# A two-layer graph network on one core: x reaches its feature-major form through VectorE, the leftover table through SyncE, both cosine tables through one pass

## The chip, the core and the metric

The kernel runs on one core of a Trainium2 chip. The metric is device time in microseconds (us), from start to end of one execution. Six queues matter here: TensorE multiplies matrices (PE in the profile; PEld is its weight load), VectorE (DVE) and ScalarE (ACT) do elementwise work and empty PSUM, GpSimd (POOL) does small elementwise work, SyncE (SP) issues most of the transfers, and 16 DMA engines carry them out. Each engine takes its instructions in a fixed order, and waits where the next one's inputs are not ready.

## The reference

128 graphs of 128 nodes with 256 features pass two layers. Only the first layer and the convolution of the second touch the change.

```python
# layer 0, x: (128 graphs, 128 nodes, 256 features), adj: (128, 128, 128)
norm  = (sum(adj, -1) + 1e-6) ** -0.5
f_hom = adj @ ((x @ theta) * norm) * norm
f_het = x @ W_h
gate  = sigmoid(x @ W_t + b_t)
x1    = layernorm(x + elu(gate * f_hom + (1 - gate) * f_het))
# layer 1
h      = relu(bn1(conv1(x1)))            # 1 tap
h      = bn2(conv2(h))                   # 17 taps along the nodes, padded by 8
x_conv = relu(h + x1)
...                                      # messages, GRU
out    = layernorm(x1 + gru(x_conv, x_nmp, x1))
```

All values are float32.

## The kernel before

The program has three stages. Stage A (lines 512 to 606) computes layer 0, conv1 and the analysis half of conv2, for 64 pairs of graphs (J = 2 graphs each). Stage B (line 702 on) multiplies by the transformed conv2 weights, stage C (line 1012 on) does the rest of layer 1. The change lies in stage A and in what is set up ahead of it.

Conv2 is done by a cosine and sine transform of length L = 136. `table` (L182) fills one table of 128x136 values per call with some twenty VectorE instructions: table A over the nodes, which the analysis (`l1_analyse`, L404) multiplies by, and table T over the taps, which turns the conv2 weights in `w_unit` (L420). The weights go through in 32 w_units of 8 features, each from four loads of 17 partitions (`w_load`, L124). The last 8 table columns ("leftovers") go another way: `way_back` (L234) copies them into tile TL in 14 small transfers, and 19 v_units (`v_unit`, L453) multiply by TL.

The stage is a software pipeline. One pass of the loop at L512, called a step here, does for pair t: `l0_project` (three products of x), the gate and elu of pair t-1, the layer norm of pair t-1 (`l0_norm`), the transposition, conv1 and analysis of the normalised x1 of pairs t-2 and t-3, and at its end `l0_turn(t+1)`, which prepares the next pair. Two units of the weights (w or v) fit into most steps; some steps have none: of the 61 steps from pair 3 on about 31 have a w_unit, 18 a v_unit, 12 neither.

A product over the features needs x with the features on the partitions. `load` (L114) brings x with the nodes on the partitions, 128 partitions of two rows of 1 KB. `l0_turn` (L293) calls `transposed` (L281): TensorE multiplies four 128x128 blocks of x by the identity into a PSUM bank, and VectorE copies the bank (128x512) to xT. After that come two transposes of the adjacency (L299), their row sum on VectorE (L301), and the power -1/2 on GpSimd (L160, L161). xT has one buffer: it is written for pair t+1 when the products of pair t have been read. The same node-major x is read again by `l0_elu` (L368) as the residual.

The order within an engine is that of the program text for TensorE always, and from step 3 on for SyncE, VectorE and ScalarE as well (`manual_schedule`, L513); for steps before that, a scheduler chooses theirs at build time, and GpSimd's always. `norm_stats` (L258) ends in two small GpSimd instructions (`inv_sqrt`) that ScalarE's normalisation (L273) needs.

```python
def transposed(src, dst, name):
    t = bank(f"{name}_ps")
    for c in range(NC):
        for j in range(J):
            nc.tensor.transpose(t[:, ...], src[:, j, c * P : (c + 1) * P], ident)
    nc.vector.tensor_copy(dst.rearrange("p c n -> p (c n)"), t)
```

Of the kernel before, what the change touches and what calls it, by code (L numbers as in the profile page):

```python
# [34 lines left out]
def gnn_layers_kernel(ctx: ExitStack, tc: tile.TileContext, a: dict, out: bass.AP):  # L35
# [47 lines left out]
    taps = actx.enter_context(tc.tile_pool(name="taps", bufs=1, side="right", reuse_waits="tile"))  # L83
    acon = actx.enter_context(tc.tile_pool(name="acon", bufs=1, side="right", reuse_waits="tile"))
    w0 = acon.tile([P, NC, 3 * D], F32, tag="w0", name="w0")
    A = acon.tile([P, M], F32, tag="A", name="A")
    S = const.tile([P, P], F32, tag="S", name="S")
    SL = const.tile([P, P], F32, tag="SL", name="SL")
    T = taps.tile([P, M], F32, tag="T", name="T")
    FS = P // TAPS  # L90
    TL = taps.tile([P, P], F32, tag="TL", name="TL")
    conv1_w = acon.tile([P, NC, D + CO], F32, tag="conv1_w", name="conv1_w")
    shift1 = acon.tile([P, D], F32, tag="shift1", name="shift1")
    NW = 3
    vt = [taps.tile([P, 2, D], F32, tag=f"vt{i}", name=f"vt{i}") for i in range(2)]
    wt = [taps.tile([P, 2, D], F32, tag=f"wt{i}", name=f"wt{i}") for i in range(NW)]
# [12 lines left out]
    def bank(name):  # L109
        return ps.tile([P, 512], F32, tag="ps", name=name)  # L110
# [2 lines left out]

    def load(p):  # L114
        s = st[p] = {}
        s["x"] = io.tile([P, J, D], F32, tag="x", name=f"x_{p}")
        nc.sync.dma_start(s["x"], x[p * J : (p + 1) * J].rearrange("b n d -> n b d"))
        s["adjT"] = io.tile([P, J, P], F32, tag="adjT", name=f"adjT_{p}")
        nc.sync.dma_start(s["adjT"], adjT[:, p * J : (p + 1) * J, :])

    QF = D // 4
    NU = QF // 2
# [9 lines left out]

    load(0)
    for j, name in enumerate(("L0_gnn_theta", "L0_gnn_W_h", "L0_gnn_W_t")):
        (nc.sync if j == 2 else nc.scalar).dma_start(
            w0[:, :, j * D : (j + 1) * D], a[name].rearrange("(c p) e -> p c e", p=P)
        )
    def rows(name, lo, hi, pool=acon):

        t = pool.tile([P, hi - lo], F32, tag=f"{name}{lo}", name=f"{name}{lo}_b")  # L140
# [38 lines left out]
    lag = as_float("lag", 1, quarters, [[0, 1]], -PAD, 1)  # L179
    step = 2.0 * math.pi / L  # L180

    def table(dst, at, name):  # L182


        def tmp(q, dt=F32):
            return setup.tile([P, M], dt, tag=f"{name}_{q}", name=f"{name}_{q}")

        v = nc.vector
        arg, r, u, w, acc = (tmp(q) for q in ("arg", "r", "u", "w", "acc"))
        turns = tmp("turns", I32)  # L190
        v.scalar_tensor_tensor(arg, freq, at, quad, ALU.mult, ALU.subtract)
        v.tensor_scalar(turns, arg, 1.0 / L, None, ALU.mult)
        v.tensor_copy(u, turns)
        v.scalar_tensor_tensor(r, u, float(-L), arg, ALU.mult, ALU.add)
        v.scalar_tensor_tensor(u, r, -1.0, r, ALU.mult, ALU.max)
        v.tensor_scalar(r, u, -1.0, float(L), ALU.mult, ALU.add)
        v.tensor_tensor(u, u, r, ALU.min)

        v.tensor_scalar(r, u, float(L // 4), -step, ALU.subtract, ALU.mult)
        v.tensor_mul(w, r, r)  # L200
        co = [(-1.0) ** i / math.factorial(2 * i + 1) for i in range(9)]
        v.tensor_scalar(acc, w, co[8], None, ALU.mult)
        for i in range(7, 0, -1):
            v.scalar_tensor_tensor(acc, acc, co[i], w, ALU.add, ALU.mult)
        v.scalar_tensor_tensor(dst, acc, 1.0, r, ALU.add, ALU.mult)


    scale = const.tile([P, 2 * NC], F32, tag="scale", name="scale")
# [25 lines left out]
    def way_back():  # L234

        AL = setup.tile([P, P // ML, ML], F32, tag="AL", name="AL")
        nc.vector.tensor_copy(AL, A[:, P:M].unsqueeze(1).to_broadcast([P, P // ML, ML]))
        nc.vector.memset(TL, 0.0)

        for t in vt:  # L240
            nc.vector.memset(t[96:], 0.0)
        back = setup.tile([P, 1], F32, tag="back", name="back")
        nc.vector.memset(back, 2.0 / L)
        nc.vector.memset(back[0:2], 1.0 / L)

        cols = TL[:, 0 : ML * FS].rearrange("p (r i k) -> p r i k", r=2, i=FS)
        for i in range(FS):
            for r in range(2):
                nc.gpsimd.dma_start(
                    cols[i * TAPS : (i + 1) * TAPS, r, i, :], T[0:TAPS, P + r : M : 2]  # L250
                )
        tS = bank("S_ps")
        nc.tensor.transpose(tS[:, 0:P], A[:, 0:P], ident)
        nc.tensor.transpose(tS[:, P : 2 * P], AL.rearrange("p a b -> p (a b)"), ident)
        nc.vector.tensor_scalar(S, tS[:, 0:P], back, None, ALU.mult)
        nc.vector.tensor_scalar(SL, tS[:, P : 2 * P], 2.0 / L, None, ALU.mult)

    def norm_stats(src, n, name):  # L258

# [26 lines left out]
                nc.tensor.transpose(  # L286
                    t[:, (c * J + j) * P : (c * J + j + 1) * P],
                    src[:, j, c * P : (c + 1) * P], ident,
                )
        nc.vector.tensor_copy(dst.rearrange("p c n -> p (c n)"), t)  # L290


    def l0_turn(p):  # L293
        s = st[p]
        s["xT"] = wf.tile([P, NC, J * P], F32, tag="xT", name=f"xT_{p}")
        transposed(s["x"], s["xT"], f"xT_{p}")
        adj = bank(f"adj_ps_{p}")
        for j in range(J):
            nc.tensor.transpose(adj[:, nodes(j)], s["adjT"][:, j, :], ident)  # L299
# [176 lines left out]
    m_in = []  # L476

    def m_load(i):
        t = io.tile([P, J, D], F32, tag="x", name=f"mx1T_{i}").rearrange("p j d -> p (j d)")
# [23 lines left out]
        return add, send  # L503


    units = {2 + u * (NP - 3) // (NU - 1): u for u in range(NU)}
    rest = [t for t in range(4, NP - 1) if t not in units]
    units_v = {rest[v * (len(rest) - 1) // (NV - 1)]: v for v in range(NV)}
# [3 lines left out]
    for t in range(-1, NP):  # L512
        with tc.manual_schedule(engines={E.PE, E.SP, E.DVE, E.Activation} if t > 2 else {E.PE}):  # L513

            def on(q, work):
                if 0 <= q < NP:
                    work(q)

            def between():
                on(t - 1, l0_gate)  # L520
                on(t - 3, l1_analyse)

            def beside():
                on(t - 1, l0_elu)

            on(t - 2, l1_turn)
            l0_project(t, between, beside) if t >= 0 else between()
            on(t - 1, l0_norm)
            if t == 0:
                norms = batch_norms()  # L530
                next(norms)
                table(A, node, "A")
                table(T, lag, "T")

                cos, sin = T[:, 2:M:2], T[:, 3:M:2]
                both = setup.tile([P, M // 2 - 1], F32, tag="both", name="both")
                nc.vector.tensor_sub(both, sin, cos)
                nc.vector.scalar_tensor_tensor(sin, sin, -1.0, cos, ALU.mult, ALU.subtract)
                nc.vector.tensor_copy(cos, both)
            on(t - 2, l1_front)  # L540
            on(t - 2, l1_store)
            if t + 2 < NP:
                if 2 <= t + 2:
                    load(t + 2)
                if 0 <= t < 2:
                    w_load(t)
                if 2 <= t < 4:
                    v_load(t - 2)
            else:
                m_load(t + 2 - NP)  # L550
            if t - 1 in units:
                w_store(units[t - 1])
            if t - 1 in units_v:
                v_store(units_v[t - 1])
            on(t + 1, l0_turn)
            if t == 3:
                nc.scalar.dma_start(w_msg, a["w_msgT"].rearrange("(c p) e -> p c e", p=P))
                nc.scalar.dma_start(b_msg, a["L1_gnn_b_msg"].partition_broadcast(P))
            if t == 1:
                next(norms, None)  # L560
                way_back()
                sctx.close()
                hpool = hstack.enter_context(tc.tile_pool(name="hpool", bufs=1))
                H = hpool.tile([P, NC, M, NB], F32, tag="H", name="H")
            on(t, l0_mix)
            if t in units_v:
                v_unit(units_v[t])
                if units_v[t] + 2 < NV:
                    v_load(units_v[t] + 2)
            if t in units:  # L570
                if units[t] + 2 < NU:
                    w_load(units[t] + 2)
                if t + 1 < NP:
                    w_unit(units[t])
# [511 lines left out]
```

## Time and profile before

| | |
|---|---|
| time, median of 3 runs (lowest to highest) | 2027.63 us (2027.56 to 2027.9) |
| the profiled execution: its own time, its span | 2027.4 us, 2025.6 us |
| stage A, by the last conv1 and analysis before the first product of stage B | 0 to about 715 us |
| TensorE, VectorE, ScalarE, GpSimd busy, share of the span | 98%, 72%, 37%, 32% |
| DMA packets, bytes | 198043, 243.02 MB |
| idle time of TensorE with a named cause, the two longest | 11.1 us, 4.4 us |

The span is what the profiler saw between the first and the last instruction; 1.8 us of the execution lie around it, and the profiled execution stands 0.2 us below the median. Busy time of TensorE is modelled at its end, since its instructions overlap, so that 98% says that it hardly ever waits and not that it works at its peak. In the timeline, an entry such as "x4" is four instructions in a row; its start is that of the first, and the next entry's start tells more of the pace than its own duration does.

### The profile page before, as it was taken

To read this page: it belongs to the slowest core of one execution; us is meant where nothing else is said; L and a number is where in the kernel's file an instruction comes from. 1 tells how busy PE (TensorE), PEld (TensorE's weight loads), DVE (VectorE), ACT (ScalarE), POOL (GpSimd) and SP (SyncE) were. 2 spreads that over 40 slices of the span, in tenths; PEclk is the share of its full clock that TensorE was granted. 3 is DMA by queue.
4 is the path that set the end of the run, shared out by engine and by line. 5 is a ranking of instruction groups with operands and counts; after the bars stand their busy time and mean duration, and the time that the engine had idled before them with its cause. 6 is when DMAs were issued, how large, how long until landed. Compare 5 with 4: busy or idle time off the path is not lost.

```text
span 2025.6 us, 26703 instructions
## 1 busy us (share of the span) xinstructions
PE 1993.2 (98%) x8679; PEld 1372.1 (68%) x8679; DVE 1461.8 (72%) x2884; ACT 746.2 (37%) x1488; POOL 645.5 (32%) x869
## 2 busy tenths in 40 slices
PE   6999999999999999999999999999999999999997
PEld 4676677677676788886666666666666666666664
DVE  6878878788788764456777677777767677776766
ACT  2565665656656611122223222222223222232222
POOL 4111111111111145543434243233424333343431
PEclk8999999999999999999999999999999999999999
DMA  5544444444443489983222122222221221221100
GB/s 102 178 160 155 141 162 149 153 159 148 158 153 132 152 301 351 324 292 118 68 69 80 61 66 80 63 64 64 80 69 58 80 78 49 65 79 47 42 27 21
DMA packets 198043, 243.02 MB, mean 120 GB/s; under 512 B 16768, under 2 KB 141456, under 8 KB 197904
## 3 DMA queue, kind: packets, MB, share of 16 engines
q1 hardware_dynamic: 190880, 235.47, 35.4%
q10 hardware_dynamic: 6352, 5.78, 0.9%
q0 software_dynamic: 672, 0.06, 0.5%
q8 instruction: 70, 1.15, 0.2%
q14 instruction: 69, 0.57, 0.1%
HBM read 136.33 MB, written 104.86 MB: 119 GB/s over the span
## 4 chain that ended last, share of the span: by engine, by line
PE 96%; DVE 1%; POOL 1%; DMA 0%; ACT 0%; issue 0%; SPq 0%; POOLq 0%; DVEq 0%; ACTq 0%
PE g_ps L970 42%; PE f_ps L319 11%; PE y_ps L711 6%; PE gate_ps L324 5%; PE conv_ps L389 5%; PE msg_ps L847 5%; PE coef_ps L409 3%; PE nmp_ps L903 3%; PE conv_ps L811 3%; PE z_ps L724 3%; PE mix_ps L345 3%; PE w_ps L425 2%; PE x1T_ps L286 2%; PE xT_ps L286 1%; PE conv_ps L818 1%; PE wl_ps L456 1%
## 5 line engine op out<-in xcount | busy, mean ns | idle before, releaser
L319 PE MATMUL f_ps<-w,xT 128*128 128x512 f32 x512 | 243.8, 599 | 0.4 <-DVE xT L290 0.4
L160 POOL TENSOR_SCALAR rstd_b<-mv_b 128x2 f32<-128x2 f32 (+1 forms) x65 | 12.5, 192 | 529.9 <-DVE mv_b L264 529.9
L929 ACT ACTIVATE o<-o 128x1024 f32<-128x1024 f32 (+1 forms) x65 | 67.8, 1044 | 268.5 <-DVE o L1006 261.7
L970 PE MATMUL g_ps<-t_h,sh 128*128 128x384 f32 x384 | 156.8, 490 | 0.0
L970 PE MATMUL g_ps<-t_c,sc 128*128 128x384 f32 x384 | 155.2, 486 | 0.0
L970 PE MATMUL g_ps<-t_m,sm 128*128 128x384 f32 x384 | 155.2, 486 | 0.0
L273 ACT ACTIVATE y<-y,nb_b,rstd_b 128x256 f32<-128x256 f32 x128 | 70.0, 593 | 219.0 <-DVE nb_b L271 215.1
L324 PEld LDWEIGHTS gate_ps<-w,xT 128*128 128x128 f32 x512 | 97.8, 191 | 68.6 <-issue 61.9
L160 POOL TENSOR_SCALAR rstd_a<-mv_a 128x2 f32<-128x2 f32 x64 | 12.3, 192 | 403.8 <-DVE mv_a L264 282.7
L324 PE MATMUL gate_ps<-w,xT 128*128 128x256 f32 x512 | 131.9, 380 | 0.0
L319 PEld LDWEIGHTS f_ps<-w,xT 128*128 128x128 f32 x512 | 88.8, 192 | 63.5 <-issue 62.3
L1003 POOL TENSOR_TENSOR u<-u,p 128x512 f32<-128x512 f32 x63 | 79.8, 1267 | 162.4 <-DVE p L987 162.4
L711 PE MATMUL y_ps<-wb,H 128*128 128x256 f32 x544 | 128.5, 379 | 0.8 <-issue 0.8
L328 ACT ACTIVATE hom<-f_ps,norm 128x256 f32<-128x256 f32 x128 | 60.7, 474 | 168.7 <-PE f_ps L319 166.0
L389 PE MATMUL conv_ps<-conv_w,x1T 128*128 128x259 f32 x512 | 122.5, 381 | 0.0
L719 POOL TENSOR_TENSOR ws<-wb 128x512 f32<-128x512 f32 x67 | 93.6, 1397 | 89.8 <-PE z_ps L724 51.5
L711 PEld LDWEIGHTS y_ps<-wb,H 128*128 128x128 f32 x544 | 103.2, 190 | 15.2 <-issue 1.3
L847 PE MATMUL msg_ps<-w_msg,cx1T 128*128 128x256 f32 x480 | 108.7, 379 | 0.0
L970 PEld LDWEIGHTS g_ps<-t_c,sc 128*128 128x128 f32 x384 | 73.0, 190 | 50.9
L970 PEld LDWEIGHTS g_ps<-t_m,sm 128*128 128x128 f32 x384 | 73.0, 190 | 50.9
L389 PEld LDWEIGHTS conv_ps<-conv_w,x1T 128*128 128x128 f32 x512 | 97.1, 190 | 14.7 <-ACT w_o L429 0.2
L970 PE MATMUL g_ps<-w_hhT_w,cx1T 128*128 128x384 f32 x256 | 105.1, 492 | 0.0
(229 smaller groups left out, 4515.4 us busy)
## 6 DMA issues: line engine op xcount, KB each, us to landing
wb<-w_d SPq DMA_DIRECT2D x68, 512.0 KB
w_d<-w_o SPq DMA_DIRECT2D x256, 128.0 KB
y_d<-yb SPq DMA_DIRECT2D x68, 256.0 KB
x<-in_x SPq DMA_DIRECT2D x64, 256.0 KB
cx1T<-x1T_d SPq DMA_DIRECT2D x64, 256.0 KB
yt<-y_d SPq DMA_DIRECT2D x32, 512.0 KB
cx<-x_d SPq DMA_DIRECT2D x32, 512.0 KB
x_d<-x SPq DMA_DIRECT2D x63, 256.0 KB
```

The costliest lines, as they stand in the source:

```text
L273: nc.scalar.activation(dst[:, q, :], src[:, q, :], AF.Identity, bias=nb[:, q : q + 1], scale=rstd[:, q : q + 1],)
L286: nc.tensor.transpose(t[:, (c * J + j) * P : (c * J + j + 1) * P], src[:, j, c * P : (c + 1) * P], ident,)
L319: nc.tensor.matmul(pf, lhsT=xT[:, c, nodes(j)], rhs=w0[:, c, 0 : 2 * D], start=(c == 0), stop=(c == NC - 1),)
L324: nc.tensor.matmul(pg[:, j * D : (j + 1) * D], lhsT=xT[:, c, nodes(j)], rhs=w0[:, c, 2 * D : 3 * D], start=(c == 0), stop=(c == NC - 1),)
L345: nc.tensor.matmul(pm[:, j * D : (j + 1) * D], lhsT=adjT_[:, j, :], rhs=hom[:, j, :], start=True, stop=True,)
L389: nc.tensor.matmul(ph[:, 0 : D + CO], lhsT=s["x1T"][:, c, nodes(j)], rhs=conv1_w[:, c, :], start=(c == 0), stop=(c == NC - 1),)
L711: nc.tensor.matmul(py[:, blk, :], lhsT=coefs(blk if k == 0 else 2 * k + 1 - blk, c), rhs=w[:, c, blk, :], start=(c == 0), stop=(c == NC - 1),)
L719: nc.gpsimd.tensor_tensor(ws, w[:, :, 0, :], w[:, :, 1, :], ALU.add)
L847: nc.tensor.matmul(pm[:, j * D : (j + 1) * D], lhsT=x1T[:, c, nodes(q)], rhs=w_msg[:, c, :], start=(c == 0), stop=(c == NC - 1),)
L929: nc.scalar.activation(rz, rz, AF.Tanh, scale=0.5)
L970: nc.tensor.matmul(pg[:, lo : lo + 3 * P], lhsT=s[f"f{kind}"][i][:, pr, :], rhs=factors[kind][i], start=(k == 0), stop=(k == 2), skip_grou ...
L1003: nc.gpsimd.tensor_tensor(u4, u2, p5, add)
```

## The change

x is loaded a second way. `load` now makes a tile xb: four transfers, one for each 64 features, each to 32 partitions, put on partition i of the quarter q the 64 features of every node whose number is i modulo 32 (8 pieces of 64 values, 256 bytes each, per partition). One VectorE instruction transposes the 32x32 blocks of xb into xT; TensorE's four transposes, the PSUM bank and the copy are gone from `l0_turn`. The feature that comes to lie on a partition is another than before, so the rows of w0 (theta, W_h, W_t) are placed to match, by four transfers for each weight in place of one. The node-major x, which `l0_elu` still reads, is loaded by `load_x` at step t, two steps later than before. xb and x have two buffers each in place of four of x.

A and T become two halves of one tile AT2 and are filled by one chain of VectorE instructions over 272 columns; the first instruction alone is done twice. `l0_turn(1)` moves ahead of the table in the text. The 14 transfers to TL leave `way_back` and GpSimd's queue: SyncE issues 7 in step 2 and 7 in step 3 (`leftover_table`). Seven products of a tile of ones come at the very start of TensorE's order.

```diff
-    A = acon.tile([P, M], F32, tag="A", name="A")
+    AT2 = acon.tile([P, 2, M], F32, tag="AT2", name="AT2")
+    A, T = AT2[:, 0, :], AT2[:, 1, :]
-    T = taps.tile([P, M], F32, tag="T", name="T")
+    K, Q = 32, P // 32
+    WARM = 7
...
     def load(p):
         s = st[p] = {}
-        s["x"] = io.tile([P, J, D], F32, tag="x", name=f"x_{p}")
-        nc.sync.dma_start(s["x"], x[p * J : (p + 1) * J].rearrange("b n d -> n b d"))
+        xb = s["xb"] = io.tile([P, J * Q, 2 * K], F32, tag="xb", bufs=2, name=f"xb_{p}")
+        for q in range(Q):
+            nc.sync.dma_start(
+                xb[q * K : (q + 1) * K],
+                x[p * J : (p + 1) * J, :, 2 * K * q : 2 * K * (q + 1)].rearrange(
+                    "b (r i) d -> i (b r) d", i=K
+                ),
+            )
         s["adjT"] = io.tile([P, J, P], F32, tag="adjT", name=f"adjT_{p}")
         nc.sync.dma_start(s["adjT"], adjT[:, p * J : (p + 1) * J, :])
+
+    def load_x(p):
+        s = st[p]
+        s["x"] = io.tile([P, J, D], F32, tag="x", bufs=2, name=f"x_{p}")
+        nc.sync.dma_start(s["x"], x[p * J : (p + 1) * J].rearrange("b n d -> n b d"))
...
-        (nc.sync if j == 2 else nc.scalar).dma_start(
-            w0[:, :, j * D : (j + 1) * D], a[name].rearrange("(c p) e -> p c e", p=P)
-        )
+        for q in range(Q):
+            (nc.sync if j == 2 else nc.scalar).dma_start(
+                w0[q * K : (q + 1) * K, :, j * D : (j + 1) * D],
+                a[name][2 * K * q : 2 * K * (q + 1)].rearrange("(c i) e -> i c e", i=K),
+            )
...
-        v.scalar_tensor_tensor(arg, freq, at, quad, ALU.mult, ALU.subtract)
+        for k, at in enumerate(ats):
+            v.scalar_tensor_tensor(parts[:, k, :], freq, at, quad, ALU.mult, ALU.subtract)
...
-        cols = TL[:, 0 : ML * FS].rearrange("p (r i k) -> p r i k", r=2, i=FS)
-        for i in range(FS):
-            for r in range(2):
-                nc.gpsimd.dma_start(
-                    cols[i * TAPS : (i + 1) * TAPS, r, i, :], T[0:TAPS, P + r : M : 2]
-                )
+    def leftover_table(half):
+        cols = TL[:, 0 : ML * FS].rearrange("p (r i k) -> p r i k", r=2, i=FS)
+        for i in range(FS):
+            nc.sync.dma_start(
+                cols[i * TAPS : (i + 1) * TAPS, half, i, :], T[0:TAPS, P + half : M : 2]
+            )
...
-        transposed(s["x"], s["xT"], f"xT_{p}")
+        nc.vector.transpose(
+            s["xT"].rearrange("p c (b i) -> p c b i", i=K),
+            s["xb"].rearrange("p b (c i) -> p c b i", c=NC),
+        )
...
+    warm = bank("warm_ps")
+    for _ in range(WARM):
+        nc.tensor.matmul(warm[:, 0:P], lhsT=ones, rhs=ones, start=True, stop=True)
...
-                table(A, node, "A")
-                table(T, lag, "T")
+                l0_turn(1)
+                table(AT2, (node, lag))
...
+            if t >= 0:
+                load_x(t)
             if t + 2 < NP:
...
                 if 2 <= t < 4:
+                    leftover_table(t - 2)
                     v_load(t - 2)
...
-            on(t + 1, l0_turn)
+            if t != 0:
+                on(t + 1, l0_turn)
```

More of the change, by code (lines that the diff above doesn't have):

```diff
@@ L180, in gnn_layers_kernel, with table @@
     step = 2.0 * math.pi / L
-    def table(dst, at, name):
+    def table(dst, ats):
         def tmp(q, dt=F32):
-            return setup.tile([P, M], dt, tag=f"{name}_{q}", name=f"{name}_{q}")
+            t = setup.tile([P, len(ats), M], dt, tag=f"table_{q}", name=f"table_{q}")
+            return t.rearrange("p k m -> p (k m)"), t
         v = nc.vector
-        arg, r, u, w, acc = (tmp(q) for q in ("arg", "r", "u", "w", "acc"))
-        turns = tmp("turns", I32)
-        v.scalar_tensor_tensor(arg, freq, at, quad, ALU.mult, ALU.subtract)
+        (arg, parts), (r, _), (u, _), (w, _), (acc, _) = (
+            tmp(q) for q in ("arg", "r", "u", "w", "acc")
+        )
+        turns, _ = tmp("turns", I32)
+        for k, at in enumerate(ats):
+            v.scalar_tensor_tensor(parts[:, k, :], freq, at, quad, ALU.mult, ALU.subtract)
         v.tensor_scalar(turns, arg, 1.0 / L, None, ALU.mult)
@@ L204, in table @@
             v.scalar_tensor_tensor(acc, acc, co[i], w, ALU.add, ALU.mult)
-        v.scalar_tensor_tensor(dst, acc, 1.0, r, ALU.add, ALU.mult)
+        v.scalar_tensor_tensor(
+            dst.rearrange("p k m -> p (k m)"), acc, 1.0, r, ALU.add, ALU.mult
+        )
     scale = const.tile([P, 2 * NC], F32, tag="scale", name="scale")
@@ L256, in way_back @@
         nc.vector.tensor_scalar(SL, tS[:, P : 2 * P], 2.0 / L, None, ALU.mult)
+    def leftover_table(half):
[3 more added lines that the diff above has]
+                cols[i * TAPS : (i + 1) * TAPS, half, i, :], T[0:TAPS, P + half : M : 2]
+            )
     def norm_stats(src, n, name):
@@ L295, in l0_turn @@
         s["xT"] = wf.tile([P, NC, J * P], F32, tag="xT", name=f"xT_{p}")
-        transposed(s["x"], s["xT"], f"xT_{p}")
+        nc.vector.transpose(
+            s["xT"].rearrange("p c (b i) -> p c b i", i=K),
+            s["xb"].rearrange("p b (c i) -> p c b i", c=NC),
+        )
         adj = bank(f"adj_ps_{p}")
@@ L478, in m_load @@
     def m_load(i):
-        t = io.tile([P, J, D], F32, tag="x", name=f"mx1T_{i}").rearrange("p j d -> p (j d)")
+        t = io.tile([P, J, D], F32, tag=("xb", "x")[i // 2], bufs=2, name=f"mx1T_{i}")
+        t = t.rearrange("p j d -> p (j d)")
         nc.sync.dma_start(t.rearrange("p (c n) -> p c n", c=NC), x1T_d[EP[i]])
```

## The prediction

> **What bounds the kernel now.** I read the waits of TensorE first. They name, in order, what was waited for, the total us, how often, the longest.
>
> ```profile
> PE x1T_ps L286 <- ACT x L273: 11.6, 3, 11.1
> PE xT_ps L286 <- DMA x<-in_x: 4.4, 1, 4.4
> ```
>
> TensorE waits for almost nothing but one gap of 11.1 us. Everywhere else its own instructions set the time, so an instruction taken from it is worth its pace. The timeline around the gap shows whose fault it is.
>
> ```profile
> 16.85 14.90 POOL L249 DMA_DIRECT2D TL<-T  x14
> 31.83 0.19 POOL L160 TENSOR_SCALAR rstd_a<-mv_a 128x2 f32<-128x2 f32 x1
> 32.85 0.16 DVE L271 SCALAR_TENSOR_TENSOR nb_a<-mv_a,rstd_a 128x2 f32<-128x2 f32 x1 [8.87 <-POOL rstd_a L161]
> 33.05 1.09 ACT L273 ACTIVATE x<-hom,nb_a,rstd_a 128x256 f32<-128x256 f32 x2 [10.11 <-DVE nb_a L271]
> 33.70 1.40 PE L286 MATMUL x1T_ps<-ident,x 128*128 128x128 f32 x4 [11.09 <-ACT x L273]
> 34.89 3.62 PE L319 MATMUL f_ps<-w,xT 128*128 128x512 f32 x4
> ```
>
> GpSimd issues the 14 TL transfers for 14.9 us, and the first layer norm's rstd_a stands behind them. After the gap TensorE is slow too: four f_ps products take 3.42 us start to start against 1.72 in a settled step. Third, a settled step, one without a weight unit, where x1T comes soonest:
>
> ```profile
> 109.42 0.60 PE L286 MATMUL xT_ps<-ident,x 128*128 128x128 f32 x4
> 109.62 0.42 DVE L393 TENSOR_TENSOR h<-conv_ps,shift 128x256 f32<-128x256 f32 x1 [0.38 <-PE conv_ps L389]
> 109.86 0.38 PE L299 MATMUL adj_ps<-ident,adjT 128*128 128x128 f32 x2
> 110.06 0.69 DVE L290 COPY xT<-xT_ps 128x512 f32<-128x512 f32 x1
> ...
> 111.38 1.88 PE L319 MATMUL f_ps<-w,xT 128*128 128x512 f32 x4
> ```
>
> The four transposes hold TensorE 0.44 us (109.42 to 109.86). The copy starts when VectorE has finished h, not when the transposes end, and finishes at 110.75; f_ps follows at 111.38, so 0.63 us is to spare. The stretches of three successive steps (no unit, w_unit, v_unit) give busy time by engine, granted clock and DMA share:
>
> ```profile
> 110.06:119.86 9.80, 9.80 (x48) 7.25 (x47) 8.26 (x19) 5.35 (x14) 1.77 (x4) 1.00 0.32 105
> 119.86:130.87 11.01, 11.01 (x56) 7.47 (x55) 8.41 (x18) 7.52 (x18) 1.77 (x4) 1.00 0.55 184
> 130.87:141.53 10.66, 10.66 (x50) 7.63 (x49) 8.98 (x19) 5.45 (x14) 1.77 (x4) 1.00 0.40 123
> 45.48:685.78 640.30, 640.30 (x3042) 447.93 (x3041) 513.05 (x1099) 388.73 (x903) 106.08 (x240) 1.00 0.47 154
> ```
>
> TensorE is full in each; VectorE, the third figure, is the next one.
>
> **The transposes in the settled part.** From pair 3 on, 61 steps lose four TensorE transposes at 0.109 us each: 61 x 0.436 = **26.6 us**. The mean step falls from 640.3 / 60 = 10.67 to 10.23 us (no unit 9.36, w 10.58, v 10.22).
>
> **The VectorE transpose** takes the copy's place in VectorE's order. No row shows one. From below: L361, 433 ns, a 128x512 pass from SBUF. From above: the set-up row L227 does one 128x128 shape in 0.28 to 0.87 us, a factor 3.1, which on 0.69 gives 2.15. I take **0.69**, that of the copy it replaces and of most 128x512 passes here (676 to 692). VectorE's own need per step is its busy time plus two waits that don't shrink with TensorE's work: 0.70 for the exp (L362) and up to 0.52 for rstd. That is 8.26 + 0.70 + 0.52 = 9.48 without a unit, 8.41 + 0.70 + 0.18 = 9.3 with a w, 8.98 + 0.70 + 0.33 = 10.0 with a v; over 12, 31 and 18 steps the mean is 9.54. TensorE's 10.23 stays above it. Only the steps without a unit come within 0.1 us, and their slack ahead of f_ps shrinks from 0.63 to 0.63 - 0.44 = 0.19, so nothing stalls. If the transpose takes 0.69 + d, VectorE becomes the bound at d = 0.69 (1.38 us), and every 0.1 us beyond costs 6.1 us.
>
> The page "VectorE: DVE Perf Modes" (section The three transpose paths) gives 311 ns for a 128x128 two-byte block on VectorE and recommends TensorE for such a size; no row here shows either. Four times 311 ns are an estimate of 1.24 us, by which the steps without a unit would run 0.64 us over TensorE's 9.36, some 5 us in all after their slack, and the sum would be about 2000.
>
> **The transfers of xb.** 1024 pieces of 256 bytes per step, 64 on each of 16 DMA engines. The records of the trace in stage A have 46 ns (median) for 1024 bytes, 85 for 2048, 9 for 4; later 27 for 512. A line through them gives 18 ns for 256 bytes. From above: q0, the TL queue, took 0.5% of 16 engines for 672 packets, 241 ns each.
>
> ```profile
> q1 hardware_dynamic: 190880, 235.47, 35.4%
> q0 software_dynamic: 672, 0.06, 0.5%
> ```
>
> At 18 ns it is 1.15 us per engine and step on top of 0.47 x 10.67 = 5.0, of 10.23: hidden. It would bound the step at (10.23 - 5.0) / 64 = 82 ns per piece. At 241 ns a step would be 5.0 + 15.4 = 20.4 us. I take 18, since sizes on either side of 256 lie on that line and q0 was filled by GpSimd one small transfer at a time.
>
> The page "DMA: Bandwidth & Descriptors" (Specifications) sets 512 bytes as the least size at line rate, below which a transfer reads, modifies and writes. No row shows such a doubling; an estimate of 36 ns from it leaves 7.3 us of 10.23, and the same sum.
>
> SyncE's queue issues four more DMAs per step, at 0.42 for x: 1.7 us. Past them move adjT, the w_d stores, wt and the x_d store of the next step. In a w step the stores end near 322.3 and x_d is issued at 323.53; it becomes some 0.5 us late, which nobody feels within the 10 us until x1 is overwritten. With a v_unit, SyncE is free for 1.2 us ahead of x_d. xb is issued a whole step ahead of its reader; x for the elu is now issued about 12 us ahead. With less lead than 3 us a late x would stop VectorE at L368, and behind it the layer norm. The TL transfers, 7 in each of two steps at 0.33 (the shortest SyncE issue) to 1.07 us (GpSimd's), hold SyncE 2.3 to 7.5 us, where it stands idle from 36.2 to 46.7 now.
>
> **The set-up.** On VectorE the order of the changed program is: xT(0), the table, the gate of pair 0, T's three finishing steps, diag and scale, xT(1). A table instruction over 136 columns takes 298 ns; from the 128x256 and 128x512 rows (0.42, 0.69) a column costs 1.06 ns, so 272 columns take 0.44. A and T alternated at 0.21 each, so a pair cost 0.42: the merge saves nothing. It costs, because in the old order xT(1) came out at 13.83 amid the table and now comes last. Working: xb(0) lands near 5.0 (x landed at 4.45; three more issues at 0.45 while the weights share the engines), xT(0) 5.7, two first instructions and the row sum 6.7, 18 chained ones at 0.36 to 0.44 (7.6) 14.3, gate 15.0, col, the 1.3 of GpSimd's scale and the diag rows 17.8, xT(1) 18.5. The products of pair 1 run 5.1 us to 23.7. In their shadow VectorE does hom (0.9), three gate rows (1.8), exp (0.9), elu (1.4), stats and gate of pair 1 to 26.4; rstd 1.0, nb 0.2, ScalarE's first half 0.6 with its hand-over: x1T of pair 0 at 28.4 in place of 33.70. **5.3 us** gained. Bounds: 2 us if the four-piece loads of x and w0 (six more issues ahead of ScalarE's table load, 2.7 us) are late by 3; 8 if xT(1) overlaps the table after all.
>
> The gap on TensorE shrinks from 11.1 to about 2.9 us. After the long one TensorE lost 3.0 us over x1T, f and gate (0.76 + 1.71 + 0.54); the granted clock from 20 to 40 us was 0.66. After a wait of 1.82 us near 710 the same kind of product ran at its usual pace. 2.9 lies between: half, **1.5 us**. WARM's seven products fill TensorE's first 4.45 us, in which it waits; if xb came earlier than they end, they would cost up to 3 us. No engine after 715 us sees the change.
>
> **Sum.** Against the profiled span: 2025.6 - 26.6 - 5.3 - 1.5 = 1992.2; I allow 1 us for steps without a unit in which VectorE's 0.1 us add up: 1993. What lies around the span (1.8) and the 0.2 to the median go on top: **1995 us**.
>
> **The rivals.** *VectorE fills up* (the transpose takes 1.2 to 1.5 us). For it: 80% busy now. Against: every comparable row is 0.69. At 1.24 it costs 5 us, at 1.5 some 9 us: 2000 to 2004. *The set-up gives nothing* (18 chained instructions and late loads eat the 6.8 us): 2027.6 - 26.6 + 1 = 2002. For it: xT(1) does fall 4.7 us back. Against: rstd no longer stands behind 14.9 us. *Slower, by a slow transpose*: at 2.15 us, the upper bound, VectorE needs 9.54 + 1.46 = 11.0 per step against 10.67 now, 61 x 0.33 = 20 us more, less 5 of the set-up: 2043; it decides from 1.93 us on. For it: the L227 spread, and a permuted read. Against: that spread appears only in set-up. *Slower, by the pieces*, from 82 ns on: at 100 ns a step is 11.4, 2067; least likely.
>
> **How the numbers follow.** Forecast 0.62, VectorE filling up 0.16, set-up giving nothing 0.10, slow transpose 0.08, slow pieces 0.04. The likeliest alone runs from 1991 (set-up 8, the full 3.0 of the clock) to 1999 (set-up 2, no clock). With the two middle rivals the range is 1990 to 2004. A measurement of this kernel tells 0.2% (4 us) from no change; the two slower cases hold 0.12, of which 0.02 would end within 4 us; faster 0.87.
>
> **What would show it.** Right: no xT_ps on TensorE, a step of 9.4, 10.2 and 10.6 us, a VectorE transpose near 0.69, x1T of pair 0 near 28 us, no 11 us gap. Wrong: f_ps waiting for VectorE's xT in most steps (the transpose is slow), xT waiting for a DMA (the pieces), or x1T of pair 0 after 32 us.

## The result, and the profile after

The changed kernel takes **2045.08 us** (median; 2041.69 to 2046.67, 4 runs) against 2027.6 for the kernel before on the same chip: a ratio of 1.0085, 95% interval 1.0067 to 1.0102. It is 17 us slower, where 33 us less were forecast. The profiled execution took 2044.01 us, its span is 2042.2, the mean granted clock 0.992 (before: 0.995).

The chain of work that ended last, of the kernel after (its shares by engine):

```profile
PE 85%; DMA 7%; DVE 3%; ACT 3%; SPq 1%; issue 1%; POOL 0%; ACTq 0%; POOLq 0%; DVEq 0%
```

A store now sets part of the end. The waits (us in total, times, longest) name it: the store of x1 to memory, x_d.

```profile
ACT x L298 <- DMA x_d<-x: 49.0, 24, 7.7
PE x1T_ps L311 <- ACT x L298: 36.1, 19, 9.9
PE f_ps L347 <- DVE xT L321: 3.1, 1, 3.1
```

x1 has one buffer. ScalarE's norm of a pair (L298) may write it only when the x1 of the pair before has been stored; TensorE's transposes of x1 wait for the norm. The VectorE transpose (last line) delays TensorE once, at the start. One stalled step, from the timeline of the kernel after (start us, duration us; in brackets the idle time before and what ended it):

```profile
283.24 1.67 SPq L143 DMA_DIRECT2D wt<-in_conv_wT  x4
285.02 1.02 SPq L429 DMA_DIRECT2D x_d<-x  x1
286.14 0.37 SPq L430 DMA_DIRECT2D x1T_d<-x1T  x1
...
288.38 0.16 DVE L296 SCALAR_TENSOR_TENSOR nb_a<-mv_a,rstd_a 128x2 f32<-128x2 f32 x1 [0.18 <-POOL rstd_a L179]
289.60 0.70 DVE L321 STREAM_TRANSPOSE xT<-xb 128x512 f32<-128x512 f32 x1
292.47 1.09 ACT L298 ACTIVATE x<-hom,nb_a,rstd_a 128x256 f32<-128x256 f32 x2 [3.61 <-DMA x_d<-x]
293.12 0.33 PE L311 MATMUL x1T_ps<-ident,x 128*128 128x128 f32 x1 [2.82 <-ACT x L298]
```

The previous norm ended at 280.78. Its store was issued 4.2 us later, at 285.02, behind the four loads of convolution weights (wt), and the next norm, whose inputs were there at 288.54, got x1 at 292.4. The chain of waits in this stretch has the store itself:

```profile
285.02 7.37 DMA x_d<-x
```

Why does a store of 256 KB take 7.37 us? The records of the DMA packets, counted by size for each microsecond of the kernel after, tell. wt moves in 136 packets of 1 KB, x_d and x1T_d in 128 packets of 2 KB each.

```
from us        283  284  285  286  287  288  289  290  291  292
1024 bytes      54    8   17   23   23  252   29   21    5   33
2048 bytes       0    0    0   79  161    0    0    0   10    6
```

At 286 and 287 the 1 KB packets come at 23 per us, one every 43 ns, and such a packet takes 46 ns: **one DMA engine** carries all of wt, while the others have next to nothing. 240 of the 256 packets of both stores, 15/16 of them, pass at 286 to 288. The last 16 follow singly, 80 ns apart, from 291.25 to 292.47: the share of that one engine, which still had wt in front of it. So a load on 17 partitions holds one engine for 34 x 46 ns = 1.6 us, four of them for 6.3 us, and whatever is issued right behind them ends that much later. The landings in the trace say the same. The four wt loads land one after the other, at 286.93, 288.54, 290.24 and 291.82 us, some 1.6 us apart. The store x_d reports sixteen landings: fifteen from 287.52 to 287.74, the last at 292.39. The same crawl is in the trace of before (22 to 24 packets per us from 312 to 317 us). There it hurt nobody: x_d was issued 0.03 us after its norm (mean of pairs 4 to 60) and had a whole step to land.

The Trainium skill has the rule behind this row: the page "DMA: Bandwidth & Descriptors", section "Why a DMA increments its semaphore by 16 and not by 1", says that a transfer is spread over the largest number of engines, up to 16, that divides the size of the slowest dimension on both of its sides. For 17 that is 1, which is what the packets show; the prediction had not weighed it.

SyncE suffers too. What it waited for from 100 to 680 us in the kernel after, the two largest entries:

```profile
SPq L122 <- DMA wt<-in_conv_wT: 32.0, 41, 1.5
SPq L129 <- DMA wt<-in_conv_wT: 31.6, 26, 1.9
```

It stops at the xb loads (L122) and the adjT load (L129) until a wt load is through, though they share no data. The trace tells why, since it names the semaphore (the counter) that each transfer waits for and the one that it counts up on landing. The program as built has eight such semaphores for the transfers of SyncE and ScalarE together and deals them out in turn. A transfer is issued only when the last one on its semaphore, eight places earlier in the program's order, has landed; so it is for all 848 transfers of the kernel after from 100 to 680 us. Here the last two xb loads and adjT stand eight places behind the last three wt loads, which land at 288.54, 290.24 and 291.82 us; they are issued at 288.55, 290.26 and 291.83. The kernel before has the eight semaphores too, but its SyncE waited for VectorE's and ScalarE's results, the two largest entries of the same stretch, and that was idle time:

```profile
SPq L402 <- DVE x1T L290: 110.1, 55, 2.9
SPq L401 <- ACT coords L396: 98.1, 51, 6.2
```

The mean delay from the end of a norm to the issue of x_d (pairs 4 to 60) grew from 0.03 to 3.48 us, at most 6.41.

The early steps lose as well. SyncE's and ScalarE's timelines of the kernel after, around the longest gap:

```profile
34.35 4.91 SPq L279 DMA_DIRECT2D TL<-AT  x7
...
51.01 5.91 SPq L279 DMA_DIRECT2D TL<-AT  x7
56.96 0.89 SPq L477 DMA_DIRECT2D vt<-in_conv_wT  x2
57.90 5.13 SPq L464 DMA_DIRECT2D w_d<-w_o  x8
63.12 1.68 SPq L143 DMA_DIRECT2D wt<-in_conv_wT  x4
64.89 1.59 SPq L429 DMA_DIRECT2D x_d<-x  x1
```

```profile
50.11 1.08 ACT L298 ACTIVATE x<-hom,nb_a,rstd_a 128x256 f32<-128x256 f32 x2
72.94 1.09 ACT L298 ACTIVATE x<-hom,nb_a,rstd_a 128x256 f32<-128x256 f32 x2 [7.71 <-DMA x_d<-x]
```

x1 was ready at 51.2; its store left at 64.89, 13.7 us late, behind TL, the w_d stores and wt, and took 8 us more. TensorE stood still for 9.87 us.

| x1T comes on TensorE | before | after | forecast |
|---|---|---|---|
| of pair 0 | 33.70 us | 27.77 us | 28.4 us |
| of pair 3 | 68.46 us | 73.59 us | some 62 us (28.4 + the 34.8 of before - the 1.5 of the clock) |
| mean step, pairs 3 to 61 | 10.67 us | 10.88 us | 10.23 us |
| undisturbed steps without unit, with w, with v | 9.85, 10.96, 10.71 | 9.42, 10.52, 10.27 | 9.36, 10.58, 10.22 |

(A step has one weight unit at most, a w or a v.) The span is 49 us over the forecast 1993: 12 up to pair 3, and 58 x 0.65 = 38 in the steps behind. Where no store is late the steps have the forecast length.

### The profile page after: what moved, and what is told of

The parts are those of the page before. It is cut to its first block, busy times and chain, and to the rows that moved or that the text cites. A ratio compares the mean times of both kernels' runs of the same rounds, so it can differ in the third digit from the quotient of the medians.

```text
span 2042.2 us, 26597 instructions
## 1 busy us (share of the span) xinstructions
PE 1981.7 (97%) x8437; PEld 1349.0 (66%) x8437; DVE 1449.2 (71%) x2867; ACT 747.7 (37%) x1488; POOL 630.2 (31%) x855
## 4 chain that ended last, share of the span: by engine, by line
PE 85%; DMA 7%; DVE 3%; ACT 3%; SPq 1%; issue 1%; POOL 0%; ACTq 0%; POOLq 0%; DVEq 0%
PE g_ps L1007 42%; PE f_ps L347 8%; PE y_ps L748 5%; DMA x_d<-x 5%; PE msg_ps L884 5%; PE gate_ps L352 4%; PE conv_ps L417 3%; PE nmp_ps L940 3%; PE conv_ps L848 3%; PE z_ps L761 3%; PE coef_ps L437 2%; PE mix_ps L373 2%; PE x1T_ps L311 1%; PE w_ps L453 1%; ACT x L298 1%; PE conv_ps L855 1%
## 5 line engine op out<-in xcount | busy, mean ns | idle before, releaser
L347 PE MATMUL f_ps<-w,xT 128*128 128x512 f32 x512 | 249.9, 612 | 3.1 <-DVE xT L321 3.1
L298 ACT ACTIVATE y<-y,nb_b,rstd_b 128x256 f32<-128x256 f32 x128 | 70.0, 593 | 219.1 <-DVE nb_b L296 219.1
```

Of the source, the lines that this page charges most:

```text
L298: nc.scalar.activation(dst[:, q, :], src[:, q, :], AF.Identity, bias=nb[:, q : q + 1], scale=rstd[:, q : q + 1],)
L347: nc.tensor.matmul(pf, lhsT=xT[:, c, nodes(j)], rhs=w0[:, c, 0 : 2 * D], start=(c == 0), stop=(c == NC - 1),)
```

## The experiments

Unless told otherwise a kernel is the changed one with the edit shown. Ratios are to the kernel before on the same chip, with the 95% interval; the last three columns are from the profiled execution of each.

| kernel | us, median | ratio | x1T of pair 0 | of pair 3 | mean step |
|---|---|---|---|---|---|
| changed kernel | 2045.08 | 1.0085 (1.0067 to 1.0102) | 27.77 | 73.59 | 10.88 |
| no_xb | 2005.70 | 0.9894 (0.9877 to 0.9910) | 30.10 | 71.64 | 10.27 |
| xd_ahead_of_wt | 2036.54 | 1.0048 (1.0033 to 1.0063) | 28.30 | 73.59 | 10.77 |
| xd_on_scalar | 2134.65 | 1.0532 (1.0516 to 1.0548) | 27.62 | 72.91 | 12.47 |
| wt_split | 2021.23 | 0.9971 (0.9961 to 0.9981) | 28.77 | 72.06 | 10.56 |
| tl_on_gpsimd | 2042.46 | 1.0075 (1.0058 to 1.0092) | 34.93 | 77.60 | 10.75 |
| wt_wide | 2003.12 | 0.9879 (0.9864 to 0.9894) | 29.19 | 69.42 | 10.27 |
| wt_wide_tl_on_gpsimd | 2008.11 | 0.9903 (0.9888 to 0.9918) | 36.16 | 74.14 | 10.27 |
| before_wt_wide | 2026.62 | 0.9997 (0.9988 to 1.0006) | 34.40 | 67.86 | 10.67 |
| before_tl_on_sync | 2023.51 | 0.9983 (0.9974 to 0.9992) | 25.75 | 65.52 | 10.67 |
| wide_xd_on_scalar | 2033.59 | 1.0037 (1.0025 to 1.0050) | 28.22 | 68.50 | 10.79 |
| wide_tl_on_scalar | 2005.24 | 0.9891 (0.9876 to 0.9905) | 29.90 | 68.98 | 10.28 |
| wide_early_xd_on_scalar | 2006.74 | 0.9897 (0.9883 to 0.9912) | 29.91 | 64.91 | 10.42 |
| wide_without_tl | 1998.90 | 0.9865 (0.9849 to 0.9882) | 27.73 | 63.64 | 10.26 |

### Is it the xb loads at all? (no_xb)

The loads of xb are left out from pair 4 on; the first layer then takes x of pair 3 for its products in every later pair.

```diff
-        xb = s["xb"] = io.tile([P, J * Q, 2 * K], F32, tag="xb", bufs=2, name=f"xb_{p}")
-        for q in range(Q):
+        if p < 4:
+            s["xb"] = io.tile([P, J * Q, 2 * K], F32, tag="xb", bufs=2, name=f"xb_{p}")
+        else:
+            s["xb"] = st["xb"]
+        xb = st["xb"] = s["xb"]
+        for q in range(Q if p < 4 else 0):
```

> The changed kernel without the four xb transfers from pair 4 on: xT of these pairs is made from the xb of pair 3, so from there on the products are those of another pair; every instruction of TensorE, VectorE, ScalarE and GpSimd stays. All three theories that blame the transfers (queue: SyncE is too full and issues the x_d store late; ring: the x_d store lands late because its pieces stand behind the wt loads on the same DMA engines; load: the DMA engines as a whole are too busy) expect the 32 us of the prediction back: 1993 to 1998 us, and ScalarE's wait for the x_d store (49 us) gone. The rival that the VectorE transpose or the new order of the compute engines costs the time expects 2040 to 2047.

2005.70 us. x_d is issued 0.03 us after its norm again (at most 0.3), no norm after 100 us waits for it, and the steps are 9.42, 10.52 and 10.27 us. So the settled loss comes of the four loads in SyncE's queue, not of the VectorE transpose, which is still there. The time is still 8 us above the 1993 to 1998 expected, because the early loss stays: x1T of pair 3 comes at 71.64. The loads of pairs 0 to 3 are still made here, so this run says nothing on their part in it.

### Which part of it: SyncE's time, or what lies in front of x_d? (xd_ahead_of_wt, xd_on_scalar, wt_split)

The store of x1 ahead of the wt and vt loads in SyncE's order:

```diff
             on(t, l0_mix)
+            if 3 <= t - 1 < NP - 2:
+                l1_store_x(t - 1)
             if t in units_v:
```

> The changed kernel with one store moved: from pair 3 on SyncE issues the x_d store of a pair at the end of the step that made x1, ahead of the loads of wt and vt of that step, and not behind them. The same transfers, the same number. Ring: the store lands some 5 us earlier, 1995 to 2002 us. Queue: it is issued 1.7 us earlier in steps with a wt load and that much of each late norm comes back, 2015 to 2030. Load: nothing, 2040 to 2047.

The store of x1 issued by ScalarE, right behind the norm:

```diff
             on(t - 1, l0_norm)
+            if 3 <= t - 1 < NP - 2:
+                nc.scalar.dma_start(x1_d[t - 1], st[t - 1]["x1"].rearrange("p j e -> p (j e)"))
```

> The changed kernel with the x_d store of pairs 3 to 61 issued by ScalarE right behind the norm that writes x1, in ScalarE's own DMA queue, and not by SyncE. Queue and ring both expect the wait for the x_d store gone: 1994 to 2000 us, some 0.35 us of ScalarE per step, hidden. Load: the store is still slow among full DMA engines, 2030 to 2047.

Each wt load as one of 16 partitions and one of a single partition, four issues more:

```diff
-            nc.sync.dma_start(
-                t[32 * r : 32 * r + TAPS], a["conv2_wT"][f : f + 2].rearrange("i t o -> t i o")
-            )
+            src = a["conv2_wT"][f : f + 2].rearrange("i t o -> t i o")
+            for lo, hi in ((0, 16), (16, TAPS)):
+                nc.sync.dma_start(t[32 * r + lo : 32 * r + hi], src[lo:hi])
```

> The changed kernel with each wt load of 17 partitions cut into one of 16 and one of 1 partition: the same bytes, four more issues of SyncE per w_unit (some 1.4 us), but the 16-partition part can spread over 16 DMA engines. Ring: the x_d store no longer stands behind 6 us of wt pieces on one engine, 1995 to 2010 us. Queue: SyncE is fuller, 2047 to 2065. Load: 2040 to 2050.

The last is the cleanest. SyncE has more to issue, x_d leaves later than ever (6.35 us behind its norm in the mean, 3.48 in the changed kernel), and yet 24 us come back, though not the 35 and more that the theory of the crowded engine ("ring") expected. A late issue alone is not what costs; what lies on the DMA engine in front of the store is. The two moves of x_d met no theory's time. With x_d ahead of wt it lands in time (the norms wait 0.6 us for it from 100 to 680 us, though it leaves 4.34 us behind them in the mean), but only 9 us come back. With x_d on ScalarE the kernel got 90 us slower, and the wait that took its place is in the waits of xd_on_scalar:

```profile
DVE x1T L315 <- DMA x1T_d<-x1T: 101.9, 25, 6.9
ACT x L298 <- DMA x_d<-x: 7.0, 1, 7.0
```

x1T, the transposed x1, has one buffer and a store of its own, still on SyncE behind wt. VectorE's copy (L315) waits for it, up to 6.9 us, and everything VectorE has behind the copy waits too. The same wait stands in xd_ahead_of_wt, 22.8 us in 13 times. Two stores stood behind wt, and I had moved one. SyncE's waits for transfers eight places earlier add to it: from 100 to 680 us 60 us for wt in xd_ahead_of_wt, and in xd_on_scalar 35 us for wt and 146 us for the very x_d that ScalarE now issues; the next section but one shows how.

### The one-engine load spread, nothing else (wt_wide, and the control before_wt_wide)

```diff
+            n = 32 if (f + 1) * TAPS + 32 <= D * TAPS else TAPS
+            w = a["conv2_wT"]
             nc.sync.dma_start(
-                t[32 * r : 32 * r + TAPS], a["conv2_wT"][f : f + 2].rearrange("i t o -> t i o")
+                t[32 * r : 32 * r + n],
+                bass.AP(tensor=w.tensor, offset=w.offset + f * TAPS * D, ap=[[D, n], [TAPS * D, 2], [1, D]]),
             )
```

> The changed kernel with each conv-weight load widened from 17 to 32 partitions (the rows behind the 17 are read and never used): as many issues in the same places, nearly twice the bytes. Theory A (a 17-partition load goes through one DMA engine, 34 packets at 46 ns = 1.6 us, 6.3 us for four; x_d, issued behind, waits for it, and ScalarE's norm for x_d): spread over the engines the loads take under 0.3 us each, ScalarE's waits for x_d in the later steps go, and the time falls by at least what the split loads gave, 24 us: 2005 to 2021. Rival B (SyncE's queue simply has too many issues for a step): same issues, same time, 2040 to 2048, and x_d is still issued 3 us and more behind its norm.

> The kernel before with the same widened conv-weight loads. Theory A (there SyncE's queue has idle time, 228 us over 118 waits for VectorE and ScalarE, the four loads have drained when x_d is issued, and x_d is issued 0.03 us after its norm): no change, 2025 to 2030. Rival B (the one-engine loads cost the kernel before as well, so that the widening is a gain of its own, not a repair of the change): 2005 to 2020.

**2003.12 us**, 42 us below the changed kernel, 2 us below theory A's range, and faster than the kernel before by 1.2%. The issues, their places and their order are the same, and the bytes are more. A store in this kernel, by the same counts of packets: x_d issued at 285.77, all its 128 packets at 286 to 288. The norms wait for it in the early steps alone, and the chain is TensorE's again:

```profile
ACT x L301 <- DMA x_d<-x: 3.4, 2, 2.1
```

```profile
PE 96%; DVE 2%; ACT 1%; DMA 1%; issue 0%; POOL 0%; SPq 0%; ACTq 0%; POOLq 0%; DVEq 0%
```

From 100 to 680 us TensorE is busy all the time here, and 558 of 580 us in the kernel after. Each view's line gives the stretch, its length, busy time (instructions) of PE, PEld, DVE, ACT and POOL, granted clock, DMA share, GB/s:

```profile
100.00:680.00 580.00, 558.13 (x2500) 378.79 (x2499) 447.17 (x979) 346.53 (x804) 94.78 (x214) 0.99 0.58 175
```

```profile
100.00:680.00 580.00, 580.00 (x2653) 400.12 (x2652) 470.74 (x1038) 366.41 (x852) 99.77 (x225) 1.00 0.62 189
```

The first is of the kernel after, the second of wt_wide: the faster one moves more bytes per second. SyncE's waits for wt are gone as well; x_d is still issued 1.65 us late in the mean, and nobody feels that. The control shows that the edit is no gain of its own: in the kernel before it changes nothing that can be measured, since there SyncE issues x_d at once. It takes both, SyncE late by the xb loads and a slow engine in front of the store.

### With the loads spread, x_d on ScalarE once more (wide_xd_on_scalar)

Both edits of above together.

> The changed kernel with the 32-partition conv-weight loads, and x_d of pairs 3 on issued by ScalarE right after the norm that writes it. Theory A (the 2135 us of x_d on ScalarE with 17-partition loads came of the one-engine loads, which then held up xb): with the loads spread the steps stay at 9.4, 10.5 and 10.3 us, mean 10.2 to 10.35, 2000 to 2008. Rival B (a store issued by ScalarE is itself what costs, whatever lies on the engines): mean step above 11, 2050 and more.

101 us of the 2134.65 come back, so most of that miss was the one-engine loads, but 30 us over wt_wide remain: neither theory's time. What SyncE waited for from 100 to 680 us in this kernel, its three largest entries:

```profile
SPq L122 <- DMA x_d<-x: 63.3, 26, 4.4
SPq L134 <- DMA x_d<-x: 35.9, 9, 5.1
SPq L468 <- DMA x_d<-x: 23.3, 10, 4.2
```

SyncE stands at loads and stores that have nothing to do with x1 (xb, x, w_d) until ScalarE's store has landed, and so x1T_d is late: VectorE waits for it 38.0 us in 21 times, and never in wt_wide. It is the eight semaphores again, which ScalarE's transfers share. One such place, from the timelines of wide_xd_on_scalar:

```profile
296.29 0.49 SPq L122 DMA_DIRECT2D xb<-in_x  x1
...
297.53 0.33 ACTq L567 DMA_DIRECT2D x_d<-x  x1
```

```profile
299.55 1.43 SPq L122 DMA_DIRECT2D xb<-in_x  x2
```

The second of the four xb loads has the semaphore that x_d had before it. SyncE had come to it at 296.8 and issued it at 299.55, when ScalarE had finished its norm and issued x_d at 297.53, and x_d had landed at 299.53. A transfer on another engine's queue stays in SyncE's way, and SyncE then waits for that engine's arithmetic as well.

### The early loss: the TL transfers

Back on GpSimd and in `way_back` as in the kernel before, without and with the wide loads:

```diff
+        for half in range(2):
+            leftover_table(half)
...
-            nc.sync.dma_start(
+            nc.gpsimd.dma_start(
...
-                    leftover_table(t - 2)
```

> The changed kernel with the fourteen transfers of the leftover table (TL) issued by GpSimd's queue right after the table is computed, as in the kernel before, and the rest as changed. Theory A (the early loss, step 0 to 3, is made by these transfers: 4.9 and 5.9 us of SyncE's queue in steps 2 and 3, ahead of x_d, which was issued 13.7 us after its norm): x1T of pair 3 comes at 65 to 69 us instead of 73.6, the later steps keep their 10.88, and the time is 6 to 9 us below the changed kernel: 2035 to 2040. Rival B (the one-engine conv-weight loads and the xb loads make the early loss as they make the later one): x1T of pair 3 stays at 71 to 74, time 2042 to 2048.

> Both edits. If the early loss is the table's transfers and the later one the one-engine loads, the gains add: x1T of pair 3 at 65 to 69 us, mean step 10.2 to 10.4, 1995 to 2012, faster than the kernel before. If both act through one thing (SyncE's queue fed late), the second edit adds under 3 us to the better of the two.

The kernel before with TL alone moved to SyncE, by the lines of the change:

```diff
-                nc.gpsimd.dma_start(
...
+            nc.sync.dma_start(
+                cols[i * TAPS : (i + 1) * TAPS, half, i, :], T[0:TAPS, P + half : M : 2]
+            )
...
                 if 2 <= t < 4:
+                    leftover_table(t - 2)
```

> The kernel before with nothing changed but the fourteen TL transfers, issued by SyncE in steps 2 and 3, seven in each, as in the changed kernel. Theory A (the early x1T of pair 0 in the changed kernel, 27.8 us, comes of this move alone, because rstd no longer stands behind 14.9 us of GpSimd's issuing, and the late x1T of pair 3 comes of it too, because x_d of pairs 1 and 2 stands behind the transfers on SyncE): x1T of pair 0 at 26 to 29 us, of pair 3 at 64 to 70 us instead of 68.46, the settled steps unchanged, 2022 to 2029. Rival B (the early loss needs the xb loads as well): x1T of pair 3 at 60 to 63, 2019 to 2022.

On ScalarE, and on SyncE with the early x_d on ScalarE:

```diff
         for i in range(FS):
-            nc.sync.dma_start(
+            nc.scalar.dma_start(
```

> The changed kernel with the 32-partition loads, and the TL transfers of steps 2 and 3 issued by ScalarE instead of SyncE, after the norm of the step. Theory A (what is left over the forecast, x1T of pair 3 at 69.4 us with a gap of 4.29 us ahead of it, is x_d of pair 2 behind TL on SyncE): x1T of pair 3 at 63 to 67, 1997 to 2002. Rival B (seven issues of 0.5 to 0.7 us hold ScalarE's next hom and gate, so that TensorE waits there): 2003 to 2010.

```diff
+            if 0 <= t - 1 < 3:
+                nc.scalar.dma_start(x1_d[t - 1], st[t - 1]["x1"].rearrange("p j e -> p (j e)"))
```

> The changed kernel with the 32-partition loads, TL on SyncE as changed, and x_d of pairs 0 to 2 alone issued by ScalarE right after their norm, so that they don't stand behind TL. Theory A as above: x1T of pair 3 at 63 to 67 us, 1996 to 2002. Rival B (what makes pair 3 late is not x_d but a load or a store behind TL, xb, adjT or w_d): x1T of pair 3 stays at 68 to 71, 2001 to 2006.

Left out, so that the leftover rows' part of the transformed weights is zero:

```diff
-                    leftover_table(t - 2)
```

> The changed kernel with the 32-partition loads and without the fourteen TL transfers: the leftover table stays at zero, so the leftover rows' part of the inverse table in w_d is zero. Theory A (what is left over the forecast is SyncE's backlog of 4.9 + 9.75 us from TL in steps 2 and 3, which three other places of the transfers or of x_d only moved): x1T of pair 3 at 61 to 65 us, of pair 4 near 75, later steps 9.42, 10.52, 10.27, and 1993 to 1998. Rival B (the w_d stores, 5.1 us in a w step, fill the queue by themselves while both tables and the weights still come in): x1T of pair 3 at 67 to 70, 2000 to 2004.

I missed on GpSimd: I had counted what SyncE wins back and forgotten that rstd stands behind GpSimd's issues again. x1T of pair 0 fell back to 34.93 and 36.16 us, pair 3 came later than in any version with TL on SyncE, and with the wide loads the move cost 5 us. GpSimd's timeline in tl_on_gpsimd:

```profile
23.52 9.47 POOL L281 DMA_DIRECT2D TL<-AT  x9
33.06 0.19 POOL L178 TENSOR_SCALAR rstd_a<-mv_a 128x2 f32<-128x2 f32 x1
```

In the kernel before the move to SyncE alone brings x1T of pair 0 to 25.75 us, 8 us earlier; the early stall leaves 2.9 of them at pair 3 and 3.7 us at the end (0.9974 to 0.9992). So the early x1T of pair 0 is the work of this move, and part of it is lost again even where no xb is loaded.

With the wide loads two more arrangements were tried, TL on ScalarE and the early x_d there; neither gains. ScalarE's timeline in wide_tl_on_scalar shows the first:

```profile
18.58 5.02 ACTq L282 DMA_DIRECT2D TL<-AT  x7
23.70 0.47 ACT L359 ACTIVATE hom<-f_ps,norm 128x256 f32<-128x256 f32 x1 [6.30 <-DMA TL<-AT]
```

Issuing holds ScalarE's arithmetic, hom waits, and x_d of pair 2 still leaves behind the w_d stores and wt, at 66.16 us (66.55 in wt_wide). The time is in rival B's range, but not clear of wt_wide's (the intervals overlap). With the early x_d on ScalarE, pair 3 comes at 64.91 as theory A had it, but the step behind it takes 19.5 us and the time is not theory A's. Without the transfers pair 3 comes at 63.64, the steps from pair 5 on have their length, and the time is 1998.90, 1 us over the range that I gave. Against wt_wide the span is 3.5 us shorter, though the ratios, measured on two chips, overlap. So the 5.8 us that pair 3 loses in wt_wide come with TL: its halves hold SyncE's queue for 4.89 us in step 2 and 9.75 us in step 3, which has nothing to spare there, and x_d of pair 2 leaves at 66.55 us, against 60.77 without them. TL's own issuing is not all of it: 5.1 of the 9.75 us SyncE waits, by the eight semaphores, for two loads of ScalarE's (w_msg and its bias), and without TL it waits 7.0 us for w_msg in that step too. Of the 12 us by which the changed kernel's pair 3 is over the forecast 62, 4.2 go with the wide loads and these 5.8 with TL. None of the places tried avoided the loss; of the versions that keep the whole computation wt_wide has the lowest time, not clear of the two variants with TL or the early x_d on ScalarE.

## Why the prediction was wrong

**The step that failed** is the sentence on SyncE's queue: "x_d becomes some 0.5 us late, which nobody feels within the 10 us until x1 is overwritten". The direction was seen, and both halves were off.

- *The lateness.* 0.5 us was the slack of one w step less four issues at 0.42. Measured: 3.48 us in the mean, 6.41 at most. 1.65 us of it stay with the loads spread and are the queue's own length; the rest went with SyncE's waits for wt. Only the issue time of the four loads was priced, not that a transfer also waits for the one eight places earlier, which put xb behind the landing of wt.
- *The cover.* "Within the 10 us" took the landing of the store as short. It took 7.37 us in the stalled step, because wt, on 17 partitions, fills one DMA engine, and one sixteenth of x_d stands behind it. 4.2 late + 7.4 to land is more than the step. The trace of before already showed the crawl, at 22 to 24 packets per us. I priced the queue, and not what the queue's transfers find in front of them on the engines; the mean DMA share (0.47) says nothing of one engine.
- *TL on SyncE* was priced at 2.3 to 7.5 us "where it stands idle from 36.2 to 46.7 now". Each half took 4.9 and 5.9 us, within the bounds. But there was no idle time left in steps 2 and 3: with xb ahead of them, and vt, w_d and wt behind, they made x_d 13.7 us late. No rival named this.

**What held.** The gain forecast for TensorE is real: 9.42, 10.52, 10.27 us where nothing is late, 9.36, 10.58, 10.22 forecast. The VectorE transpose took 0.70 us (699 to 712 ns, 64 times) against 0.69, so that VectorE never became the bound. The page "VectorE: DVE Perf Modes" would have put four blocks at an estimate of 1.24 us; the measurement decides against it for this 128x512 pass. A 256-byte packet took 18 ns (median) as the line through the other sizes had it, without the doubling that the prediction had estimated from the page "DMA: Bandwidth & Descriptors" (section Specifications). x1T of pair 0 came at 27.77 us, forecast 28.4; before_tl_on_sync shows the reason given, rstd no longer behind GpSimd's transfers.

**The rivals.** The two slower ones (slow transpose, slow pieces) were about operations that turned out at their forecast price; a late store as the new wait was dismissed inside the main line and got no price of its own. That the slow transpose's 2043 us lies near the measured 2045 is chance: the transpose took 0.70 us. With the store's delay taken away (wt_wide) the span is 2000.8, 7.8 over the forecast; with TL gone too, 1997.3, 4.3 over.

## What to carry to other kernels

When a change adds issues to a queue that is not idle, follow the next store or load in that queue to its landing, and ask whose single buffer it frees; issue time and landing time add up. A transfer over 17 partitions sat on one DMA engine here, and the mean DMA share didn't show it: look for packets that come one after the other (here 23 per us at 46 ns each) in front of anything that matters. Padding such a load to 32 partitions cost nothing here and was worth 42 us, but only in the kernel that was late. Find out, too, how many transfers the built program lets fly at once: here a transfer waited for the one eight places earlier, whoever had issued it.

## What was not expected of the hardware

- A 32-partition load with nearly twice the bytes disturbs less than one of 17 partitions, by 42 us in the changed kernel.
- Splitting 17 partitions into 16 and 1 helps (24 us) even though SyncE then issues twice as many wt transfers; padding helps more (42 us).
- After the gap of 2.82 us on TensorE at 293 us four f_ps products ran in 3.23 us start to start, at a granted clock of 0.53, against 1.72 in a settled step; so a late store can cost more than its wait. The length of the gap doesn't decide it alone: after 2.15 us, at 402 us, they took 3.21, after 2.81 and 3.04 us, at 121 and 469 us, 1.72.
- A transfer issued by ScalarE holds ScalarE's arithmetic (seven TL issues for 5.02 us).
